# A graph network on one core: keys for the on-chip row picks kept in DRAM, blocks chosen by predicated copies

## The chip, the cores and the metric

The kernel runs on one core of a Trainium2 chip. The core has five engines, each with an instruction queue of its own: PE (matrix products into PSUM), DVE (vector operations), ACT (scalar operations, and it starts DMAs), POOL (it starts the indirect gathers) and SP (it starts most DMAs). The metric is the device time of one execution in microseconds. The time before is the median of three runs.

## The reference, cut to what matters

Three layers of a transformer convolution on a graph of N = 6250 nodes, with 206250 edges sorted by target node, D = 64 columns everywhere:

```python
q = x @ Wq + bq; k = x @ Wk + bk; v = x @ Wv + bv; e = edge_attr @ We
kj = k[src] + e
alpha = jnp.sum(q[dst] * kj, axis=-1) / jnp.sqrt(jnp.float32(D))
amax = jax.ops.segment_max(alpha, dst, num_segments=N)
p = jnp.exp(alpha - amax[dst])
w = p / jax.ops.segment_sum(p, dst, num_segments=N)[dst]
agg = jax.ops.segment_sum((v[src] + e) * w[:, None], dst, num_segments=N)
x = relu(agg + x @ Ws + bs)            # then a layer norm, but for the last layer
```

The last layer ends in a log-softmax, the input is added, and the sum is normalised.

## The kernel before, in words

The edges are cut into 403 chunks of 512 (T = 4 tiles of 128 edges), and four chunks are a batch, also called a unit: 100 full batches and a rest. A layer runs over its batches once. For one batch the work is:

- **fetch** (L556): SP loads the edges' attributes, 512 KB, into one of five `feat` buffers.
- **gather** (L578): for every tile of 128 edges POOL starts one indirect DMA that brings the 128 source rows of x (256 bytes each) into `feat`. A chunk's gathers are held by a small `gate` copy of its indices (L609, on ACT), made eight chunks ahead of the chunk that is being turned.
- **pick**: some tiles of a batch get their rows from the chip instead. In layer 0 an earlier sorting step has put the edges of each chunk in an order in which tile 0 holds only sources from the first RB = 18 blocks of 128 nodes, and tile 3 only from the last 18. Those blocks lie in SBUF as `parts`, split into two terms. A pick of one tile makes a one-hot and multiplies it with `parts`.
- **turn** (L1473, L1476): PE transposes a chunk's rows, and ACT copies them into `featT`.
- **scores** (L1484, L1488): PE adds a mask from the edges' position codes and the product of q and `featT` in the PSUM tile `ps_s`; DVE takes the maximum (L1498) and its negative (L1500), ACT the exponential `prob` (L1502).
- **weights** (L1510, L1512) transposes `prob` through the PSUM tile `ps_p`; **sums** (L1522, L1530) multiplies it with the rows; **store** (L1536) writes the partial result to DRAM.

A group of four node blocks is ended (`finish`: both partial results combined, output product, norm, next layer's projections) in about eight steps, one step in a batch, on DVE, PE and ACT between the other work. Layer 0 also sorts: products that permute the edge attributes (L983 makes the one-hot `hit` on DVE, L993 and L1002 multiply), `drain` (L1013, L1016, then the DMAs `toS` L1017 and `eaS` L1020 from ACT's queue), `index` (L1038: PE finds indices and block numbers of the sorted edges; DVE puts them into `src_b` and `kbs`) and the attributes transposed to `eaP`.

A pick runs so. `toS` holds for a batch 128 rows with the sorted edges' codes: position bits, and the source's node number split into h (its group of four blocks), its block within the group, and p (its row in the block). `decode` (L1608, on SP) loads this tile, 128 KB, three batches ahead. `Picker.aim` multiplies it with `coef` (L1182, one 128-column product for each pick): the product holds in every partition the key 128 h + p of each edge. One DVE operation (L1196) compares two picks' keys with `rank` in all NH = 5 groups h and gives `hot`, 128 x 5 x 256. `Picker.batch` multiplies (L1218: five groups by two terms, ten products a pick, 256 columns each but 128 for the last group) and so has for every edge the four candidate rows of its group. L1229 multiplies these with `which` (L1188, which of the four blocks it is), and two adds (L1232, L1233) put the row into `feat`. The products for keys go to PSUM tile `ps_m` in layers 1 and 2, to `ps_p` in layer 0; the candidates to one of two `ps_x` in layers 1 and 2, to the single `ps_s` in layer 0. Picks are taken two at a time, and `aim` for the next two is issued ahead of the products for the present two. `PICKS` sets how many tiles are picked: three a batch in layer 0 (one in the first ones), six in layers 1 and 2, so 13 and 10 gathers are left.

The order on each engine is the order in which the code is written: the main loop spreads picks, sorting and endings over the four turns of a batch.

Of the kernel before, what the change touches and what calls it, by code (L numbers as in the profile page):

```python
# [41 lines left out]
PICKS = ((3,), (6,), (6,))  # L42
LEAD = (4, 1, 1)


def slot(j):

    return j % 2 * (LB // 2) + j // 2
# [378 lines left out]
def main_path(  # L427
# [82 lines left out]
    tos = ctx.enter_context(tc.tile_pool(name="tos", bufs=4))  # L510
# [5 lines left out]
    gates = ctx.enter_context(tc.tile_pool(name="gates", bufs=6 * LB))  # L516
# [24 lines left out]
    toS = dram.tile([NT, P, CH], BF16, name="toS")  # L541
# [129 lines left out]
    def locate(k, m):  # L671

        half = CH // 2
        for i in range(2):
            at = slice(k * CH + i * half, k * CH + (i + 1) * half)
            room = picks.tile([P, NH, 2 * P], F32R, name="hot").rearrange("p h e -> p (h e)").bitcast(F32)
# [49 lines left out]
    fours = picks.tile([P, 2, KB, D], F32, name="rows_of_b", bufs=1).rearrange("p s b d -> p (s b d)")  # L726
# [20 lines left out]
    def widen(i):  # L747
# [3 lines left out]
        room = picks.tile([P, 2, KB, D], F32, name="rows_of_b", bufs=1).rearrange("p s b d -> p (s b d)")  # L751
# [70 lines left out]
    codeS = const.tile([P, P], BF16, name="codeS")  # L822
    coef = const.tile([P, LB, P], BF16, name="coef")
    pickc = const.tile([P, 2, LB], BF16, name="pickc")
    kbs = const.tile([P, NT, 2, LB], BF16, name="kbs")
# [3 lines left out]
    def tools():  # L829
# [4 lines left out]
        room = picks.tile([P, 2, KB, D], F32, name="rows_of_b", bufs=1).rearrange("p s b d -> p (s b d)")  # L834
        two, wide = room[:, :LB], room[:, P : 2 * P]
        at = [ident[:, i::W] for i in range(ROW_K + 1)]
        nc.vector.scalar_tensor_tensor(two, at[ROW_H], float(P), at[ROW_P], ALU.mult, ALU.add)
        nc.vector.tensor_copy(coef, two.unsqueeze(2).to_broadcast([P, LB, P]))
        nc.vector.scalar_tensor_tensor(pickc[:, 0], at[ROW_B], float(P), at[ROW_P], ALU.mult, ALU.add)
        nc.vector.tensor_copy(pickc[:, 1], at[ROW_K])  # L840
        nc.vector.memset(wide, 0.0)
        for j in range(LB):
            rows = slice(slot(j) * W, (slot(j) + 1) * W)
            nc.vector.tensor_copy(wide[rows, j * W : j * W + BITS + 1], bit[rows, :])
        pc = ps("a")
        nc.tensor.transpose(pc[:, :P], wide, ident)
        nc.vector.tensor_scalar(codeS, pc[:, :P], FAR, None, ALU.mult)
# [93 lines left out]
    class Move:  # L941
# [68 lines left out]
        def drain(self):  # L1010
# [6 lines left out]
            nc.scalar.dma_start(toS[self.k], self.to)  # L1017
# [15 lines left out]
        def index(self):  # L1033

            k = self.k
            pi = ps("a")[:, : T * 2 * LB].rearrange("p (t v c) -> p t v c", t=T, v=2)
# [15 lines left out]
            nc.vector.tensor_copy(kbs[:, k], pi[:, 0 :: T - 1, 1])  # L1052

# [99 lines left out]
    class Picker:  # L1153


        def __init__(self, layer):
            self.layer = layer
            self.todo = []
            for k in range(len(batches)):
                those = spots(picked(layer, k))  # L1160
                for t in (0, T - 1):
                    cs = [c for c, i in those if i == t]
                    self.todo += [(k, t, cs[i : i + 2]) for i in range(0, len(cs), 2)]
            self.aimed = []
            self.which = {}
            self.side = 0
            self.keys = ps("m") if layer else None

        def aim(self):

            if not self.todo or (self.layer, self.todo[0][0]) not in codes:
                return
            k, t, cs = self.todo.pop(0)
            n = len(cs)
            to = codes[self.layer, k]
            if self.layer:
                self.side = 1 - self.side
                pk = self.keys[:, self.side * 2 * P :][:, : n * P]
            else:
                pk = ps("p")[:, : n * P]  # L1180
            for s, c in enumerate(cs):
                nc.tensor.matmul(  # L1182
                    pk[:, s * P : (s + 1) * P], coef[:, c, :], to[:, t * P : (t + 1) * P], start=True, stop=True
                )
            if (self.layer, k) not in self.which:
# [9 lines left out]
            hot = picks.tile([P, NH, 2 * P], F32R, name="hot")[:, :, : n * P]  # L1195
            nc.vector.tensor_tensor(  # L1196
                hot,
                pk.unsqueeze(1).to_broadcast([P, NH, n * P]),
                rank.unsqueeze(2).to_broadcast([P, NH, n * P]),
                ALU.is_equal,  # L1200
            )
            self.aimed.append((k, t, cs, hot, self.which[self.layer, k]))

        def batch(self, k):
# [3 lines left out]
            while self.aimed and self.aimed[0][0] == k:  # L1208
                _, t, cs, hot, which = self.aimed.pop(0)
                self.aim()  # L1210
                n = len(cs)
                px = ps("x" if self.layer else "s").rearrange("p (s b d) -> p s b d", s=2, b=KB)
                b0 = RB if t else 0
                for s in range(n):
                    for m, h in enumerate((0, *reversed(range(1, NH)))):
                        w = min(KB, RB - h * KB)
                        for i in range(2):
                            nc.tensor.matmul(  # L1218
                                px[:, s, :w].rearrange("p b d -> p (b d)"),
# [5 lines left out]
                    if s + 1 < n:  # L1225
                        yield
                at = (LB if t else 0) + cs[0]
                rows = picks.tile([P, 2, KB, D], F32, name="rows_of_b", bufs=1)[:, :n]
                nc.vector.tensor_tensor(  # L1229
                    rows, px[:, :n], which[:, at : at + n, :].unsqueeze(3).to_broadcast([P, n, KB, D]), ALU.mult  # L1230
                )
                nc.vector.tensor_tensor(rows[:, :, : KB // 2], rows[:, :, : KB // 2], rows[:, :, KB // 2 :], ALU.add)  # L1232
                nc.vector.tensor_tensor(  # L1233
                    loaded[self.layer, k][:, cs[0] : cs[0] + n, t, 0], rows[:, :, 0], rows[:, :, 1], ALU.add
                )
                yield
# [176 lines left out]
    class Unit:  # L1413


        def __init__(self, layer, c, m):
# [6 lines left out]
            if self.placed:  # L1423
                self.to = codes[layer, self.k]
                return
# [406 lines left out]
```

## Time and profile before

| | |
|---|---|
| three runs | 4648.56 us median, 4645.43 to 4657.05 |
| the profiled execution | 4656.6 us; span 4654.9 us |
| granted TensorE clock | 0.966 on average |
| busy share of the span | PE 91%, DVE 82%, POOL 72%, ACT 43% |
| gathers | 3380 indirect DMAs, 0.96 us each in layers 1 and 2, 1.03 in layer 0 |
| layers 0, 1, 2 | their first gathers start at 5, 1982 and 3324 us |

A line of groups reads: source line, engine, operation, output tile <- input tiles, shapes, count | busy us in total, mean ns of one | idle time of the engine just before them, and what ended it. A timeline line reads: start us, length us, engine, line, operation, tiles, and in brackets the idle time before it with its releaser. Matmuls overlap, so their busy time is the time in which at least one is under way.

### The profile page before, as it was taken

To read this page: it belongs to the slowest core of one execution; us is meant where nothing else is said; L and a number is where in the kernel's file an instruction comes from. 1 tells how busy PE (TensorE), PEld (TensorE's weight loads), DVE (VectorE), ACT (ScalarE), POOL (GpSimd) and SP (SyncE) were. 2 spreads that over 40 slices of the span, in tenths; PEclk is the share of its full clock that TensorE was granted. 3 is DMA by queue.
4 is the path that set the end of the run, shared out by engine and by line. 5 is a ranking of instruction groups with operands and counts; after the bars stand their busy time and mean duration, and the time that the engine had idled before them with its cause. 6 is when DMAs were issued, how large, how long until landed. Compare 5 with 4: busy or idle time off the path is not lost.

```text
span 4654.9 us, 117245 instructions
## 1 busy us (share of the span) xinstructions
PE 4216.7 (91%) x41145; PEld 3111.6 (67%) x41145; DVE 3829.2 (82%) x9064; ACT 1995.7 (43%) x5733; POOL 3337.9 (72%) x3390
## 2 busy tenths in 40 slices
PE   6889999999999999689999999999699999999996
PEld 3445555555555555367888888887478778878874
DVE  6778888898888888478888888888478888888885
ACT  2455555555555555333333333333234333334443
POOL 6777777777777766277777777777477777777774
PEclk9999999999999999799999999999799999999997
DMA  8787777777777777445555565555356655656553
GB/s 188 192 210 184 188 204 188 189 195 200 199 198 193 192 197 189 125 102 132 137 139 137 138 144 138 140 138 129 86 128 143 141 135 135 138 130 143 136 135 81
DMA packets 769749, 725.47 MB, mean 156 GB/s; under 512 B 403478, under 2 KB 544880, under 8 KB 769156
## 3 DMA queue, kind: packets, MB, share of 16 engines
q1 hardware_dynamic: 572564, 480.73, 43.5%
q0 software_dynamic: 108160, 110.97, 12.7%
q10 hardware_dynamic: 88432, 126.17, 7.7%
q8 instruction: 334, 5.47, 0.5%
q14 instruction: 259, 2.12, 0.2%
HBM read 557.62 MB, written 159.87 MB: 154 GB/s over the span
## 4 chain that ended last, share of the span: by engine, by line


## 5 line engine op out<-in xcount | busy, mean ns | idle before, releaser
L578 POOL DMA_INDIRECT feat<-x,gate x2004 | 1924.4, 960 | 613.9 <-issue 471.5
L578 POOL DMA_INDIRECT feat<-in_x,gate x1328 | 1365.8, 1028 | 526.2 <-issue 317.1
L1218 PE MATMUL ps_x<-parts,hot 128*128 128x256 f32 (+1 forms) x11880 | 1567.1, 288 | 0.0
L1218 PEld LDWEIGHTS ps_x<-parts,hot 128*128 128x128 f32 x11880 | 1457.1, 193 | 0.0
L1476 ACT COPY featT<-ps_a 64x256 f32<-64x256 f32 x2380 | 872.4, 367 | 1305.8 <-PE ps_a L1473 1265.2
L1196 DVE TENSOR_TENSOR hot<-ps_m,rank 128x1280 fp32r<-128x1280 f32 x594 | 879.9, 1481 | 33.1 <-PE ps_m L1182 32.9
L993 PE MATMUL ps_x<-hit,thirds 128*64 128x512 bf16 x4800 | 637.7, 393 | 5.5 <-DVE hit L983 5.1
L1473 PE MATMUL ps_a<-ident,feat 128*128 128x128 f32 x2380 | 488.0, 283 | 64.0 <-DMA feat<-x,gate 40.4
L983 DVE TENSOR_SCALAR hit<-ruler,pos 128x512 bf16<-128x512 f16 x1600 | 504.6, 363 | 1.7 <-PE ps_m L1002 1.5
L1473 PEld LDWEIGHTS ps_a<-ident,feat 128*128 128x128 f32 x2380 | 281.9, 140 | 333.4 <-issue 287.5
L1229 DVE TENSOR_TENSOR rows_of_b<-ps_x,which 128x512 f32<-128x512 f32 x594 | 406.4, 684 | 88.1 <-PE ps_x L1218 87.1
L1502 ACT ACTIVATE prob<-ps_s,part 128x512 f32<-128x512 f32 (+1 forms) x306 | 210.6, 688 | 625.6 <-DVE part L1500 500.0
L1218 PE MATMUL ps_s<-parts,hot 128*128 128x256 f32 (+1 forms) x2680 | 392.3, 294 | 30.9 <-ACT prob L1502 30.9
L993 PEld LDWEIGHTS <-thirds 128*64 128x64 bf16 x4800 | 233.2, 111 | 230.5 <-issue 83.6
L1218 PEld LDWEIGHTS ps_s<-parts,hot 128*128 128x128 f32 x2680 | 340.8, 195 | 60.7 <-ACT prob L1502 40.7
L1498 DVE TENSOR_REDUCE most<-ps_s 128x1 f32<-128x512 f32 (+1 forms) x306 | 211.2, 690 | 189.4 <-PE ps_s L1488 181.4
L1232 DVE TENSOR_TENSOR rows_of_b<-rows_of_b 128x256 f32<-128x256 f32 (+1 forms) x776 | 321.0, 414 | 26.6
L1522 PE MATMUL ps_g<-feat,probT 128*32 128x128 f32 x9672 | 338.2, 279 | 4.1 <-DVE y L1366 2.3
L1488 PE MATMUL ps_s<-featT,q 128*32 128x512 f32 x2418 | 336.3, 611 | 5.9 <-ACT featT L1469 5.2
L1522 PEld LDWEIGHTS ps_g<-feat,probT 128*32 128x32 f32 x9672 | 263.5, 111 | 52.6 <-issue 34.0
L1512 DVE COPY probT<-ps_p 128x512 f32<-128x512 f32 (+1 forms) x306 | 209.2, 684 | 99.0 <-PE ps_p L1510 97.3
L1182 PEld LDWEIGHTS <-coef 128*128 128x128 bf16 x1456 | 134.7, 99 | 190.5 <-issue 175.1
(226 smaller groups left out, 4392.6 us busy)
## 6 DMA issues: line engine op xcount, KB each, us to landing
feat<-eaP SPq DMA_DIRECT2D x296, 512.0 KB
featT<-eaS SPq DMA_DIRECT2D x296, 512.0 KB
raw<-in_ea SPq DMA_DIRECT2D x200, 256.0 KB
eaS<-eT ACTq DMA_DIRECT2D x200, 256.0 KB
eaP<-eN ACTq DMA_DIRECT2D x200, 256.0 KB
to<-toS SPq DMA_DIRECT2D x296, 128.0 KB
feat<-x,gate POOLq DMA_INDIRECT x2004
feat<-in_x,gate POOLq DMA_INDIRECT x1328
```

Source lines behind the costliest of these rows:

```text
L578: nc.gpsimd.indirect_dma_start(out=feat[:, c, t, 0], out_offset=None, in_=xts[layer][:, :], in_offset=bass.IndirectOffsetOnAxis(ap=index[: ...
L983: nc.vector.tensor_scalar(hit, ruler, self.pos[:, at : at + 1], None, ALU.is_equal)
L993: nc.tensor.matmul(self.px[i][j * D : (j + 1) * D, :], self.thirds[i][:, part, (j * T + t) * D : (j * T + t + 1) * D], self.hits[t, 2 * i ...
L1196: nc.vector.tensor_tensor(hot, pk.unsqueeze(1).to_broadcast([P, NH, n * P]), rank.unsqueeze(2).to_broadcast([P, NH, n * P]), ALU.is_equal,)
L1218: nc.tensor.matmul(px[:, s, :w].rearrange("p b d -> p (b d)"), hot[:, h, s * P : (s + 1) * P], parts[:, i, b0 + h * KB : b0 + h * KB + w, ...
L1229: nc.vector.tensor_tensor(rows, px[:, :n], which[:, at : at + n, :].unsqueeze(3).to_broadcast([P, n, KB, D]), ALU.mult)
L1232: nc.vector.tensor_tensor(rows[:, :, : KB // 2], rows[:, :, : KB // 2], rows[:, :, KB // 2 :], ALU.add)
L1473: nc.tensor.transpose(pt[:, t // 2 * P : (t // 2 + 1) * P], rows[:, t * D : (t + 2) * D], ident)
L1476: nc.scalar.copy(featT[:, :, h, :], pt[h * D : (h + 1) * D, : T // 2 * P].rearrange("d (i e) -> d i e", e=P))
L1488: nc.tensor.matmul(self.p_s[slot(j) * W : (slot(j) + 1) * W, :], self.q[:, j * STRIDE : j * STRIDE + W], self.featT[:, j, :], start=False, ...
L1498: nc.vector.tensor_reduce(top[:n], self.p_s[:n], AX.X, ALU.max)
L1522: nc.tensor.matmul(p_g[rows, :].rearrange("n (h d) -> n h d", h=2), self.probT[:, t, rows], batch[:, c + j, t], start=(t == 0), stop=(t == ...
```

## The change

- `index` gets one more product: `keyc` (four columns) with the sorted codes gives the keys of tiles 0 and 3 of four chunks, 4 x 256. ACT copies them as fp16 and stores them in `keyS` in DRAM, 2 KB a batch.
- `decode` loads those keys of a batch, broadcast to 128 partitions (256 bytes for each pick in each partition), two or three batches ahead, behind the fourth turn. The `coef` products are gone.
- `aim` makes the one-hots of all picks of one tile kind of a batch (up to four) by five comparisons from SBUF, into two alternating buffers.
- The choice among four candidate rows is a copy of the first (on ACT in layers 1 and 2, on DVE in layer 0) and three predicated copies over it on DVE.
- `toS` keeps only the 24 rows of position codes that the scores need, written by four DMAs; each unit loads them itself, and `codeS` gives way to `codeT`.
- Picks in layers 1 and 2: 7, 6, 7 in turn. `tos` has two buffers, not four; `gates` 16, not 24.

The diff, without the three places where a scratch tile gets another name:

```diff
@@ -39,8 +39,9 @@
-PICKS = ((3,), (6,), (6,))
+PICKS = ((3,), (7, 6, 7), (7, 6, 7))
...
+MOST = max(n for p in PICKS for n in p)
@@ -507,13 +508,13 @@
-    tos = ctx.enter_context(tc.tile_pool(name="tos", bufs=4))
+    tos = ctx.enter_context(tc.tile_pool(name="tos", bufs=2))
...
-    gates = ctx.enter_context(tc.tile_pool(name="gates", bufs=6 * LB))
+    gates = ctx.enter_context(tc.tile_pool(name="gates", bufs=4 * LB))
@@ -538,7 +539,8 @@
-    toS = dram.tile([NT, P, CH], BF16, name="toS")
+    toS = dram.tile([NT, LB, BITS + 1, CH], BF16, name="toS")
+    keyS = dram.tile([NT, 2, LB, P], FP16, name="keyS")
@@ -819,10 +821,9 @@
     ones = const.tile([P, P], BF16, name="ones")
-    codeS = const.tile([P, P], BF16, name="codeS")
-    coef = const.tile([P, LB, P], BF16, name="coef")
+    keyc = const.tile([P, LB], BF16, name="keyc")
     pickc = const.tile([P, 2, LB], BF16, name="pickc")
-    kbs = const.tile([P, NT, 2, LB], BF16, name="kbs")
+    kbs = const.tile([P, NT, 2, LB], mybir.dt.uint8, name="kbs")
     four = const.tile([P, KB], F32, name="four")
@@ -831,20 +832,10 @@
         nc.vector.tensor_copy(four, ruler[:, :KB])
-        room = picks.tile([P, 2, KB, D], F32, name="rows_of_b", bufs=1).rearrange("p s b d -> p (s b d)")
-        two, wide = room[:, :LB], room[:, P : 2 * P]
         at = [ident[:, i::W] for i in range(ROW_K + 1)]
-        nc.vector.scalar_tensor_tensor(two, at[ROW_H], float(P), at[ROW_P], ALU.mult, ALU.add)
-        nc.vector.tensor_copy(coef, two.unsqueeze(2).to_broadcast([P, LB, P]))
+        nc.vector.scalar_tensor_tensor(keyc, at[ROW_H], float(P), at[ROW_P], ALU.mult, ALU.add)
         nc.vector.scalar_tensor_tensor(pickc[:, 0], at[ROW_B], float(P), at[ROW_P], ALU.mult, ALU.add)
         nc.vector.tensor_copy(pickc[:, 1], at[ROW_K])
-        nc.vector.memset(wide, 0.0)
-        for j in range(LB):
-            rows = slice(slot(j) * W, (slot(j) + 1) * W)
-            nc.vector.tensor_copy(wide[rows, j * W : j * W + BITS + 1], bit[rows, :])
-        pc = ps("a")
-        nc.tensor.transpose(pc[:, :P], wide, ident)
-        nc.vector.tensor_scalar(codeS, pc[:, :P], FAR, None, ALU.mult)
         for stamp in stamps:
@@ -1014,7 +1005,8 @@
                 nc.scalar.copy(self.eT[i], self.px[i])
-            nc.scalar.dma_start(toS[self.k], self.to)
+            for c in range(LB):
+                nc.scalar.dma_start(toS[self.k, c], self.to[c * W : c * W + BITS + 1])
             for i in range(2):
@@ -1033,7 +1025,12 @@
             k = self.k
-            pi = ps("a")[:, : T * 2 * LB].rearrange("p (t v c) -> p t v c", t=T, v=2)
+            pa = ps("a")
+            pi = pa[:, : T * 2 * LB].rearrange("p (t v c) -> p t v c", t=T, v=2)
+            pk = pa[:LB, 2 * P :].rearrange("c (t e) -> c t e", t=2)
+            nc.tensor.matmul(
+                pk, keyc, self.to.rearrange("r (t e) -> r t e", t=T)[:, :: T - 1], start=True, stop=True
+            )
             for t in range(T):
@@ -1050,6 +1047,9 @@
             nc.vector.tensor_copy(kbs[:, k], pi[:, 0 :: T - 1, 1])
+            key = small.tile([LB, 2, P], FP16, name="key", bufs=1)
+            nc.scalar.copy(key, pk)
+            nc.scalar.dma_start(keyS[k].rearrange("t c e -> c t e"), key)
@@ -1160,28 +1160,18 @@
                     cs = [c for c, i in those if i == t]
-                    self.todo += [(k, t, cs[i : i + 2]) for i in range(0, len(cs), 2)]
+                    self.todo += [(k, t, cs)] if cs else []
             self.aimed = []
             self.which = {}
-            self.side = 0
-            self.keys = ps("m") if layer else None
+            self.turn = 0
...
-            if not self.todo or (self.layer, self.todo[0][0]) not in codes:
+            if not self.todo or (self.layer, self.todo[0][0]) not in keys:
                 return
...
             n = len(cs)
-            to = codes[self.layer, k]
-            if self.layer:
-                self.side = 1 - self.side
-                pk = self.keys[:, self.side * 2 * P :][:, : n * P]
-            else:
-                pk = ps("p")[:, : n * P]
-            for s, c in enumerate(cs):
-                nc.tensor.matmul(
-                    pk[:, s * P : (s + 1) * P], coef[:, c, :], to[:, t * P : (t + 1) * P], start=True, stop=True
-                )
+            first = LB * P if t else 0
             if (self.layer, k) not in self.which:
@@ -1192,13 +1182,13 @@
                 self.which[self.layer, k] = which
-            hot = picks.tile([P, NH, 2 * P], F32R, name="hot")[:, :, : n * P]
-            nc.vector.tensor_tensor(
-                hot,
-                pk.unsqueeze(1).to_broadcast([P, NH, n * P]),
-                rank.unsqueeze(2).to_broadcast([P, NH, n * P]),
-                ALU.is_equal,
-            )
+            room = (LB, MOST - LB)[self.turn]
+            hot = picks.tile([P, NH, room * P], F32R, name=f"hot{self.turn}", bufs=1)[:, :, : n * P]
+            self.turn = 1 - self.turn
+            for h in range(NH):
+                nc.vector.tensor_scalar(
+                    hot[:, h], keys[self.layer, k][:, first : first + n * P], rank[:, h : h + 1], None, ALU.is_equal
+                )
             self.aimed.append((k, t, cs, hot, self.which[self.layer, k]))
@@ -1208,32 +1198,33 @@
                 self.aim()
-                n = len(cs)
-                px = ps("x" if self.layer else "s").rearrange("p (s b d) -> p s b d", s=2, b=KB)
                 b0 = RB if t else 0
-                for s in range(n):
+                for s, c in enumerate(cs):
+                    if s % 2 == 0:
+                        n = min(2, len(cs) - s)
+                        px = ps("x" if self.layer else "s").rearrange("p (s b d) -> p s b d", s=2, b=KB)
                     for m, h in enumerate((0, *reversed(range(1, NH)))):
...
                             nc.tensor.matmul(
-                                px[:, s, :w].rearrange("p b d -> p (b d)"),
+                                px[:, s % 2, :w].rearrange("p b d -> p (b d)"),
                                 hot[:, h, s * P : (s + 1) * P],
...
                             )
-                    if s + 1 < n:
-                        yield
-                at = (LB if t else 0) + cs[0]
-                rows = picks.tile([P, 2, KB, D], F32, name="rows_of_b", bufs=1)[:, :n]
-                nc.vector.tensor_tensor(
-                    rows, px[:, :n], which[:, at : at + n, :].unsqueeze(3).to_broadcast([P, n, KB, D]), ALU.mult
-                )
-                nc.vector.tensor_tensor(rows[:, :, : KB // 2], rows[:, :, : KB // 2], rows[:, :, KB // 2 :], ALU.add)
-                nc.vector.tensor_tensor(
-                    loaded[self.layer, k][:, cs[0] : cs[0] + n, t, 0], rows[:, :, 0], rows[:, :, 1], ALU.add
-                )
-                yield
+                    if s % 2 == n - 1:
+                        at = (LB if t else 0) + c - n + 1
+                        found = loaded[self.layer, k][:, c - n + 1 : c + 1, t, 0]
+                        copy = nc.scalar.copy if self.layer else nc.vector.tensor_copy
+                        copy(found, px[:, :n, 0])
+                        for b in range(1, KB):
+                            nc.vector.copy_predicated(
+                                found,
+                                which[:, at : at + n, b].bitcast(I32).unsqueeze(2).to_broadcast([P, n, D]),
+                                px[:, :n, b],
+                            )
+                    yield
@@ -1420,13 +1411,9 @@
             self.plain = not layer and not self.placed
-            if self.placed:
-                self.to = codes[layer, self.k]
-                return
             self.to = tos.tile([P, CH], BF16, name="to")
-            nc.sync.dma_start(
-                self.to[: m * (BITS + 1), :], places[c : c + m].rearrange("c b e -> (c b) e")
-            )
+            here = toS[self.k] if self.placed else places[c : c + m]
+            nc.sync.dma_start(self.to[: m * (BITS + 1), :], here.rearrange("c b e -> (c b) e"))
@@ -1480,10 +1467,7 @@
             self.p_s = ps("s")
-            if self.placed:
-                nc.tensor.matmul(self.p_s, codeS, self.to, start=True, stop=False)
-            else:
-                nc.tensor.matmul(self.p_s[:n], codeT[:k, :n], self.to[:k, :], start=True, stop=False)
+            nc.tensor.matmul(self.p_s[:n], codeT[:k, :n], self.to[:k, :], start=True, stop=False)
             for j in range(self.m):
@@ -1599,13 +1583,17 @@
-    codes = {}
+    keys = {}
...
-        if k < NT and placed(layer, k) and (layer, k) not in codes and (layer or k in moved):
-            codes[layer, k] = tos.tile([P, CH], BF16, name="to")
-            nc.sync.dma_start(codes[layer, k], toS[k])
+        n = picked(layer, k) if k < NT else 0
+        if n and (layer, k) not in keys and (layer or k in moved):
+            keys[layer, k] = picks.tile([P, MOST * P], FP16, name="keys", bufs=2)
+            nc.sync.dma_start(
+                keys[layer, k][:, : n * P],
+                keyS[k].rearrange("t c e -> (t c e)")[: n * P].partition_broadcast(P),
+            )
@@ -1684,8 +1672,6 @@
             chunks[layer, u + 1].across()
-            for k in range(u + 1, u + 4):
-                decode(layer, k)
             if layer:
@@ -1722,6 +1708,8 @@
             move(pace)
+            for k in range(u + 2, u + 4):
+                decode(layer, k)
```

## The prediction

> **What bounds the kernel now.** I first cut the span by stage with the table of stretches (PE, PEld, DVE, ACT, POOL busy us with instructions, then granted clock, DMA share, GB/s): a steady piece of layer 0, of layer 1 and of layer 2.
>
> ```profile
> 600.00:1800.00 1200.00, 1124.85 (x11138) 686.44 (x11134) 1046.39 (x3148) 641.71 (x1639) 864.86 (x852) 0.99 0.77 195
> 2300.00:3200.00 900.00, 858.36 (x8683) 723.58 (x8675) 783.25 (x1437) 340.50 (x1118) 683.11 (x712) 1.00 0.59 138
> 3400.00:4500.00 1100.00, 1031.94 (x10420) 877.39 (x10412) 949.99 (x1748) 430.93 (x1384) 835.02 (x869) 0.99 0.60 137
> ```
>
> PE is busy 94 to 95% in all three, DVE 86 to 87%. The groups of the layer 1 stretch (count, busy, mean ns, idle before and its releaser), POOL's and PE's:
>
> ```profile
> L578 POOL DMA_INDIRECT feat<-x,gate x712 | 683.7, 960 | 217.1 <-issue 163.8 <-DMA feat<-x,gate 28.7 <-ACT gate L609 10.4
> L1182 PE MATMUL ps_m<-to,coef 128*128 128x128 bf16 x426 | 58.4, 218 | 40.4 <-DVE hot L1196 40.0
> ```
>
> 426 coefficient products are 71 batches of six picks, so a batch takes 900/71 = 12.68 us. A gather comes every 900/712 = 1.264 us, and ten to a batch are 12.64: POOL has no free time. PE works 858.36/71 = 12.09 of the 12.68, and nearly all its idle time (40.0 of 41.6 us, 0.56 a batch) is one wait. The timeline of PE and DVE shows it:
>
> ```profile
> 2603.60 2.61 PE L1218 MATMUL ps_x<-parts,hot 128*128 128x256 f32 x20
> 2606.04 0.38 PE L1473 MATMUL ps_a<-ident,feat 128*128 128x128 f32 x2
> 2607.68 0.27 PE L1182 MATMUL ps_m<-to,coef 128*128 128x128 bf16 x2 [1.25 <-DVE hot L1196]
> ```
> ```profile
> 2603.43 0.69 DVE L1498 TENSOR_REDUCE most<-ps_s 128x1 f32<-128x512 f32 x1 [0.60 <-PE ps_s L1488]
> 2604.21 0.15 DVE L1500 TENSOR_SCALAR part<-most 128x1 f32<-128x1 f32 x1
> 2604.28 1.22 DVE L1334 TENSOR_TENSOR w<-both,mm 128x1024 f32<-128x1024 f32 x1
> 2605.53 0.69 DVE L1337 TENSOR_TENSOR w<-w 128x512 f32<-128x512 f32 x1
> 2606.14 1.48 DVE L1196 TENSOR_TENSOR hot<-ps_m,rank 128x1280 fp32r<-128x1280 f32 x1
> 2607.54 0.68 DVE L1229 TENSOR_TENSOR rows_of_b<-ps_x,which 128x512 f32<-128x512 f32 x1
> ```
>
> DVE comes to the one-hot late, because 1.86 us of a node group's ending stand ahead of it, and PE waits. So in layers 1 and 2 three things lie within 5% of each other: POOL's pace, PE's work, and this DVE lump. Fewer gathers alone cannot bring the 10 to 9.33 that the counts suggest (0.84 us a batch): PE takes the saved gathers over.
>
> Layer 0: three picks a batch, so 196 coefficient products are 65.3 batches of 18.4 us. POOL needs 13 gathers of 1.264, 16.4. From its groups and ACT's timeline:
>
> ```profile
> L1510 PE MATMUL ps_p<-ident,prob 128*128 128x128 f32 x264 | 43.3, 286 | 17.1 <-DVE hot L1196 17.1
> L1182 PE MATMUL ps_p<-to,coef 128*128 128x128 bf16 x196 | 33.7, 226 | 3.3 <-DVE probT L1512 3.1
> ```
> ```profile
> 1205.53 0.33 ACTq L1017 DMA_DIRECT2D toS<-to  x1
> 1206.02 0.84 ACTq L1020 DMA_DIRECT2D eaS<-eT  x2
> 1206.90 0.27 ACT L1530 COPY part<-ps_g 128x128 f32<-128x128 f32 x1 [0.42 <-ACT eT L1016]
> 1208.59 0.69 ACT L1502 ACTIVATE prob<-ps_s,part 128x512 f32<-128x512 f32 x1 [1.42 <-DVE part L1500]
> ```
>
> PE waits there because keys and probabilities share one PSUM buffer (ps_p). ACT has 1.84 us idle between its drain and the exponential.
>
> **Layers 1 and 2, per batch.** PE loses six coefficient products. A pair starts 0.09 us ahead of the first pick product (2603.51 to 2603.60) and lasts 0.22; I take 0.16, three pairs 0.48. PE gains two thirds of a pick: 20 products take 2.44 us (2603.60 to 2606.04), so a pick is 1.22 and the gain 0.81. PE's work becomes 12.09 - 0.48 + 0.81 = 12.42 in layer 1. In layer 2 it was 1031.94/86.9 = 11.87 (869 gathers, ten a batch) of 12.66, and becomes 12.20.
>
> The stall: today PE reaches its second group 0.25 (turn) + 2.44 + 0.25 = 2.9 us after the scores, DVE has the next one-hot at 0.85 (maximum and its negative) + F + 1.40, F being the ending's work. F over 0.65 stalls; F = 1.86 gives 1.2, the 1.25 seen. Afterwards the one-hots are made from SBUF, a half batch ahead, and what is late next is the product buffer: the third group needs the first one's selection, at 0.85 + F + 1.8 (five compares) + 1.0 (three predicated copies) = 3.65 + F, and PE comes to it at about 5.3. So F may reach 1.65. I leave 0.15 of the 0.59 in layer 1, and 0.35 of the 0.79 in layer 2, whose endings are longer. 12.57 and 12.55: -0.11 each, on 99 batches of two layers -22 us. With no stall left it is -(0.26 + 0.46) x 99 = -71; with all of it, +65.
>
> The prices in that chain. Compare (tensor_scalar with a pointer, fp16 in, four-byte out, SBUF), by duration min/median/max of two rows:
>
> ```profile
> L983 DVE TENSOR_SCALAR hit<-ruler,pos x1600: 218/345/578, 58.8 to 1910.0; 128x512 bf16<-128x512 f16 x178
> L1369 DVE TENSOR_SCALAR y<-y x39: 226/321/495, 380.1 to 4643.2; 128x256 f32<-128x256 f32 x33, 128x192 f32<-128x192 f32 x3, 128x128 f32<-128x128 f32 x3
> ```
>
> For 512 columns it lies between 0.345 (two-byte result) and 0.69 (copy of 512 f32, L1512). Where columns go one by one, one costs 1.045 ns (1481 less 812 ns, for 640 columns of L1196). The f32 row's fastest are 0.226 for its 128 columns, 0.259 for 192 and 0.293 for 256: 0.52 ns a column on 0.16; a pointer operand adds 0.055 (L1395, 64 columns, 0.247). So I take 0.48 for four picks, 0.41 for three, 0.34 for two, each about 0.05 less from start to start, since they overlap (four of 0.345 take 1.28 us at 1205.23 in layer 0). A batch: 3.6 to 4.0 against 3 x 1.48 = 4.44. The Trainium skill (VectorE: DVE Perf Modes, The perf-mode tier table) lets an fp32 tensor_scalar of SBUF run at twice the rate of an fp32 tensor_tensor or of a PSUM operand; 0.52 against 1.045 ns agrees. At the slower rate, by this page what the old form pays, the sum would be that of rival (2). Predicated copy, 128 columns: no row has one; between a 128 x 128 copy (ACT's 0.27) and twice the tensor_tensor of that size (L1233, 298 ns). I take 0.30 and the 0.03 gap of dependent instructions, eleven a batch: 3.6 against 3 x 1.41 = 4.22. The first copy goes to ACT: 3.7 x 0.27 = 1.0 us on an engine 38% busy. DVE falls from 11.03 to about 9.8.
>
> POOL: 9.33 x 1.264 = 11.80, under PE. Keys: a load of up to 0.23 MB a batch for 0.13, and one small load more, at a DMA share of 0.6: nothing. They stand on SP at a batch's end and wait for the compares of two batches earlier, done by mid-batch; behind them stands the next feat load, which waits for PE anyway. Gates 24 to 16: at most eight ahead and four in work, nothing.
>
> **Layer 0, per batch.** PE loses two coefficient groups, 0.32, their wait 0.05, and ps_p's wait 17.1/65.3 = 0.26. It gains the key product, between a pickc product (16.5/264 = 0.06) and a 512-column one (0.38): 0.15. ACT gains a copy (0.37) and four DMA issues of 0.33 to 0.42; in the built order the last of six issues in a row uses the semaphore of the first again, and so waits for its landing. Most fits into the 1.84 idle; I let 0.1 through (none, to 2). DVE drops 0.5, hidden. Net -0.38, 96 batches: -36.
>
> Sum -58 on the profiled execution's 4656.6: 4598.6. The median shown is 8.0 lower, so 4590.
>
> **Rivals.** (1) POOL stays the pace. In layer 0, where 16 fast compares a batch run beside the gathers, these average 1016 ns, not 960; 0.09 more each gives 9.33 x 1.354 = 12.64, and layers 1 and 2 gain nothing: -36, 4612. And L1369 at 256 columns takes 0.293 in layer 0, mostly 0.43 to 0.495 in layers 1 and 2, so fast compares and gathers do hold each other up. Against it: the median gather is 947 ns in both stages, and the layer 0 mean gives only 9.33 x 1.32 = 12.3, under PE's 12.4. The Trainium skill (SBUF — State Buffer, Who interferes with whom) says that such a compare locks GpSimd out of a shared port for its whole length, and the other way round; this speaks against the change, and both rows agree. (2) DVE becomes the bound. Besides one-hot and selection it has 11.03 - 8.66 = 2.4, and 0.88 of waits at scores and transposes (62.5/71) that it can't fill; the point is 9.4 us for both. Compares at one column per cycle are 6.0, with copies at 0.38 from start to start 4.2: 13.5 a batch, +155 in layers 1 and 2, less 36: 4768. With 9.7 us for both it is 4668. Copies of 0.6 alone do the same. (3) All stalls go, layer 0 keeps 0.48: -71 - 46, 4532. (4) ACT's queue eats layer 0's gain (0.6 a batch gets through instead of 0.1): -22 + 12, 4639, no change.
>
> **Numbers.** Forecast 0.38, (1) 0.20, (2) 0.20, (3) 0.12, (4) 0.10. About 0.3% (14 us) can be told from no change. Faster: forecast, (1) and (3), less 0.03 that fall short, 0.67; same 0.11; slower 0.22. The range reaches from under (3) to the lower prices of (2): 4510 to 4700.
>
> **What would show it.** Right: no PE wait for a one-hot, compares near 0.4, predicated copies near 0.3, POOL with gaps, batches of about 12.55 in layers 1 and 2 and 18.0 in layer 0. Wrong: gathers back to back with a mean over 1.0 (1); DVE over 93% busy (2); PE idle behind ACT's exponential or ps_a in layer 0 (4).

## The result, and the profile after

The changed kernel takes 4709.86 us (median of 6 runs, 4701.55 to 4722.78), the kernel before 4651.97 (6 runs): ratio 1.0126, 95% interval 1.0108 to 1.0144. So it is slower by 1.3%, where 4590 was forecast. The profiled execution took 4702.4 us, with a span of 4700.6 (before: 4654.9) and a granted clock of 0.961 (0.966). Four of the kernels below were first run in a session in which every kernel took 38% longer, the kernel before too (6420.1 us), and there one store came to 0.9952 of it, two buffers to 0.9951, four stores in the old kernel to 1.0215 and the key path to 1.0025; only the later runs of these four, labelled _2, are used.

DVE takes one maximum a batch (L1498 before, L1482 after), 306 in all, so the two traces can be laid side by side, maximum by maximum. The changed kernel is 7.0 us late at the 8th, 83.7 at the 92nd, 95.9 at the 106th, early in layer 1, 70.0 at the 204th, its end, and 45.9 at the last. Over 84 batches of each layer, in us a batch:

| | before | forecast | after |
|---|---|---|---|
| layer 0 | 18.36 | 17.98 | 19.28 |
| layer 1 | 12.68 | 12.57 | 12.42 |
| layer 2 | 12.65 | 12.55 | 12.37 |

Layers 1 and 2 gained 50 us, over twice the 22 that were forecast. Layer 0 lost 95 where it should have gained 36. The table of stretches of the kernel after (PE, PEld, DVE, ACT, POOL busy us with instructions, granted clock, DMA share, GB/s):

```profile
600.00:1800.00 1200.00, 1114.71 (x10518) 667.62 (x10518) 955.84 (x3295) 632.53 (x1626) 866.63 (x817) 0.97 0.69 180
2300.00:3200.00 900.00, 893.84 (x8877) 765.22 (x8876) 675.08 (x2094) 407.04 (x1405) 685.24 (x687) 1.00 0.61 149
3400.00:4500.00 1100.00, 1067.41 (x10599) 917.63 (x10600) 812.51 (x2545) 511.65 (x1731) 837.11 (x843) 0.99 0.60 145
```

In layer 1 PE is busy 99.3% (95.4% before) and DVE has fallen from 87 to 75%: the stall is gone. In layer 0 PE is no busier than before, gets less done (10518 products for 11138), and its clock is lower, 0.97 for 0.99. The groups of the layer 1 stretch, POOL's and DVE's:

```profile
L580 POOL DMA_INDIRECT feat<-x,gate x687 | 686.1, 999 | 215.0 <-issue 151.5 <-ACT gate L611 13.8 <-DMA feat<-x,gate 12.8
...
L1222 DVE COPY_PREDICATED feat<-which,ps_x 128x128 f32<-128x128 int32 x652 | 195.5, 301 | 119.0 <-ACT feat L1220 99.2 <-issue 3.7
L1189 DVE TENSOR_SCALAR hot<-keys,rank 128x512 fp32r<-128x512 f16 x360 | 151.6, 487 | 0.0
L1189 DVE TENSOR_SCALAR hot<-keys,rank 128x384 fp32r<-128x384 f16 x245 | 87.8, 422 | 0.0
L1189 DVE TENSOR_SCALAR hot<-keys,rank 128x256 fp32r<-128x256 f16 x120 | 37.3, 375 | 0.0
```

Compares of 0.487, 0.422 and 0.375 us and predicated copies of 0.301: the prices taken were 0.48, 0.41, 0.34 and 0.30. A gather has gone from 0.960 to 0.999. What PE waits for in that stretch (us in total, times, longest), where 40.0 us stood for the one-hot:

```profile
PE ps_x L1209 <- DVE feat L1222: 5.8, 11, 0.8
```

An ending's lump now stands ahead of compares that PE needs half a batch later, as PE's and DVE's timelines show:

```profile
2610.95 2.61 PE L1209 MATMUL ps_x<-parts,hot 128*128 128x256 f32 x20
2613.39 0.38 PE L1460 MATMUL ps_a<-ident,feat 128*128 128x128 f32 x2
2613.53 2.60 PE L1209 MATMUL ps_x<-parts,hot 128*128 128x256 f32 x20
```
```profile
2611.95 1.24 DVE L1293 TENSOR_SCALAR y<-y,mv,dev 128x64 f32<-128x64 f32 x4
2613.22 0.89 DVE L1298 TENSOR_TENSOR y<-y,gb 128x256 f32<-128x256 f32 x2
2614.03 1.81 DVE L1189 TENSOR_SCALAR hot<-keys,rank 128x256 fp32r<-128x256 f16 x5
2615.75 1.83 DVE L1222 COPY_PREDICATED feat<-which,ps_x 128x128 f32<-128x128 int32 x6
```

Layer 0 (600 to 1800 us), PE's groups for the shared buffers: the wait at L1494 (17.1 us before, L1510) is gone, but L1209 waits for the selection, and the endings' products wait for L1514, the drain of ps_g on ACT:

```profile
L1209 PE MATMUL ps_s<-parts,hot 128*128 128x256 f32 x1880 | 280.4, 298 | 35.8 <-DVE feat L1222 18.3 <-ACT prob L1486 17.5
...
L1494 PE MATMUL ps_p<-ident,prob 128*128 128x128 f32 x252 | 41.3, 286 | 0.0
...
L1268 PE MATMUL ps_g<-ws,xT 64*128 64x65 f32 x64 | 11.7, 337 | 17.3 <-ACT part L1514 17.3
...
L1354 PE MATMUL ps_g<-ve,wT 128*128 128x64 f32 x56 | 8.6, 302 | 8.6 <-ACT part L1514 8.6
```

ACT's timeline after its drain, and PE's beside it:

```profile
1202.84 0.63 ACTq L1009 DMA_DIRECT2D toS<-to  x2
...
1203.50 0.66 ACTq L1009 DMA_DIRECT2D toS<-to  x2
1204.95 1.97 ACTq L1012 DMA_DIRECT2D eaS<-eT  x2
1206.96 0.27 ACT L1514 COPY part<-ps_g 128x128 f32<-128x128 f32 x1 [3.17 <-DMA toS<-to]
1208.87 0.69 ACT L1486 ACTIVATE prob<-ps_s,part 128x512 f32<-128x512 f32 x1 [1.64 <-DVE part L1484]
```
```profile
1204.91 0.44 PE L1460 MATMUL ps_a<-ident,feat 128*128 128x128 f32 x2
1207.28 1.10 PE L1354 MATMUL ps_g<-ve,wT 128*128 128x64 f32 x8 [1.94 <-ACT part L1514]
...
1211.45 2.50 PE L1209 MATMUL ps_s<-parts,hot 128*128 128x256 f32 x10
```

The four `toS` issues take 1.3 us, then the two of `eaS` hold ACT's queue for 1.97 us (0.84 before): in this batch the second waits until the first `toS` store, whose semaphore it is to use, has landed. The drain that stands behind it starts 3.17 us after ACT's last work, and PE stands idle for 1.94 us. Then ten pick products take 2.50 us, which take 1.22 elsewhere: the clock records put TensorE at half rate from 1209.3 to 1216.1.

### The profile page after: what moved, and what is told of

The parts are those of the page before. It is cut to its first block, busy times and chain, and to the rows that moved or that the text cites. A ratio compares the mean times of both kernels' runs of the same rounds, so it can differ in the third digit from the quotient of the medians.

```text
span 4700.6 us, 121008 instructions
## 1 busy us (share of the span) xinstructions
PE 4320.8 (92%) x41108; PEld 3192.2 (68%) x41108; DVE 3447.4 (73%) x11319; ACT 2197.6 (47%) x6559; POOL 3325.4 (71%) x3258
## 4 chain that ended last, share of the span: by engine, by line
## 5 line engine op out<-in xcount | busy, mean ns | idle before, releaser
L580 POOL DMA_INDIRECT feat<-x,gate x1872 | 1862.3, 995 | 614.3 <-issue 403.1
L580 POOL DMA_INDIRECT feat<-in_x,gate x1328 | 1414.1, 1065 | 572.3 <-issue 311.8
L1209 PE MATMUL ps_x<-parts,hot 128*128 128x256 f32 (+1 forms) x13200 | 1712.9, 286 | 32.5 <-ACT feat L1220 16.6
L1209 PEld LDWEIGHTS ps_x<-parts,hot 128*128 128x128 f32 x13200 | 1604.8, 191 | 53.8 <-ACT feat L1220 32.5
L1189 DVE TENSOR_SCALAR hot<-keys,rank 128x384 fp32r<-128x384 f16 (+3 forms) x2460 | 916.4, 437 | 0.0
L1222 DVE COPY_PREDICATED feat<-which,ps_x 128x128 f32<-128x128 int32 (+1 forms) x2178 | 617.1, 288 | 377.9 <-ACT feat L1220 314.5
L984 PE MATMUL ps_x<-hit,thirds 128*64 128x512 bf16 x4800 | 650.7, 398 | 6.1 <-DVE hit L974 6.1
L1460 PE MATMUL ps_a<-ident,feat 128*128 128x128 f32 x2380 | 483.2, 284 | 31.4 <-DMA feat<-x,src_b 21.4
L1460 PEld LDWEIGHTS ps_a<-ident,feat 128*128 128x128 f32 x2380 | 280.5, 141 | 297.2 <-issue 270.9
L1220 ACT COPY feat<-ps_x 128x128 f32<-128x128 f32 (+1 forms) x726 | 186.4, 257 | 629.2 <-PE ps_x L1209 619.8
L1209 PE MATMUL ps_s<-parts,hot 128*128 128x256 f32 (+1 forms) x2680 | 404.6, 300 | 57.8 <-ACT prob L1486 33.9
L1209 PEld LDWEIGHTS ps_s<-parts,hot 128*128 128x128 f32 x2680 | 348.3, 199 | 119.9 <-issue 71.5
L984 PEld LDWEIGHTS <-thirds 128*64 128x64 bf16 x4800 | 237.1, 112 | 236.4 <-issue 89.7
L1482 DVE TENSOR_REDUCE most<-ps_s 128x1 f32<-128x512 f32 (+1 forms) x306 | 211.2, 690 | 227.7 <-PE ps_s L1472 221.1
L611 ACT COPY gate<-src_b 128x4 int32<-128x4 int32 x1185 | 227.1, 192 | 0.0
```

Source lines behind the costliest of these rows:

```text
L580: nc.gpsimd.indirect_dma_start(out=feat[:, c, t, 0], out_offset=None, in_=xts[layer][:, :], in_offset=bass.IndirectOffsetOnAxis(ap=index[: ...
L611: copy(gate, index[:, i : i + T])
L984: nc.tensor.matmul(self.px[i][j * D : (j + 1) * D, :], self.thirds[i][:, part, (j * T + t) * D : (j * T + t + 1) * D], self.hits[t, 2 * i ...
L1189: nc.vector.tensor_scalar(hot[:, h], keys[self.layer, k][:, first : first + n * P], rank[:, h : h + 1], None, ALU.is_equal)
L1209: nc.tensor.matmul(px[:, s % 2, :w].rearrange("p b d -> p (b d)"), hot[:, h, s * P : (s + 1) * P], parts[:, i, b0 + h * KB : b0 + h * KB + ...
L1222: nc.vector.copy_predicated(found, which[:, at : at + n, b].bitcast(I32).unsqueeze(2).to_broadcast([P, n, D]), px[:, :n, b],)
```

## The experiments

Theory A was that this queue makes layer 0 late. Rival B was the selection: the one ps_s is held for about 1.2 us (a copy and three predicated copies) where it was free after the multiply of 0.69. Rival C was the key product with its copy and store.

In the listings below the line numbers of the edited kernels differ by a few.

**One store of `to`** (after):

```diff
-    toS = dram.tile([NT, LB, BITS + 1, CH], BF16, name="toS")
+    toS = dram.tile([NT, P, CH], BF16, name="toS")
-            for c in range(LB):
-                nc.scalar.dma_start(toS[self.k, c], self.to[c * W : c * W + BITS + 1])
+            nc.scalar.dma_start(toS[self.k], self.to)
-            here = toS[self.k] if self.placed else places[c : c + m]
+            here = toS[self.k].rearrange("(c w) e -> c w e", w=W)[:, : BITS + 1] if self.placed else places[c : c + m]
```

> The changed kernel with the rows of `to` stored whole, in one DMA of 128 rows instead of four of six; the load picks the 24 rows out of it. Theory A (ScalarE's queue: the last of six issues in a row waits until the first has landed, the drain of ps_g behind it is late, PE stalls and its clock is halved for 3.4 us or more after it): the 143 us that L1514 waits for toS and eaS in layer 0 go, half-clock time in layer 0 falls from 177 us towards 102, and layer 0 gives back 60 to 95 of the 94 us it lost: 4615 to 4650 us. Theory B (the selection holds ps_s for 1.2 us instead of 0.69, so PE's next pick products are late): no change, 4700 to 4715. Theory C (key product, its copy and its store): 4700 to 4715.

Measured: 4648.62 us (ratio to before 0.9985, 0.9976 to 0.9995), 61 us less than the change; layer 0 18.66 us a batch. No wait of the drain for `toS` or `eaS` is left, and PE's wait for the drain falls from 30.5 to 1.3 us in layer 0. Half-clock time, counted from the third to the 98th maximum, falls from 150 to 106 us (before: 75). Theory A holds for two thirds of the loss.

**Two product buffers in layer 0** (after):

```diff
-                        px = ps("x" if self.layer else "s").rearrange("p (s b d) -> p s b d", s=2, b=KB)
+                        px = ps("x" if self.layer else "sp"[s // 2]).rearrange("p (s b d) -> p s b d", s=2, b=KB)
```

> The changed kernel with the third pick's products of layer 0 put into ps_p instead of ps_s, so that they need not wait for the selection of the first two. Theory A: at most the 24 us that PE waits there for L1222, and little of it in the end, since ACT is late anyway: 4685 to 4710. Theory B: the 24 us and the half-clock time behind them, 40 to 70 us: 4640 to 4670. Theory C: no change.

Measured: 4703.31 (1.0105, 1.0082 to 1.0128), 7 us less than the change, less than the two intervals tell apart. Half of the wait for the selection only changes its place, to L1494, and PE waits for DVE elsewhere, at L984, as well:

```profile
PE ps_x L984 <- DVE hit L974: 21.2, 29, 1.1
...
PE ps_p L1494 <- DVE feat L1222: 12.9, 21, 0.6
```

Rival B, as a matter of that buffer, falls: of its 24 us of waits little is got back. What the selection costs layer 0 as a whole, this run does not show.

**Four stores in the kernel before:**

```diff
-            nc.scalar.dma_start(toS[self.k], self.to)
+            for c in range(LB):
+                nc.scalar.dma_start(toS[self.k, c * W : (c + 1) * W], self.to[c * W : (c + 1) * W])
```

> The kernel before with its one store of `to` made four of 32 rows each (the same bytes). Theory A: the wait appears in the old kernel too, and layer 0 loses 50 to 95 us: 4700 to 4745, layers 1 and 2 as before (12.67 us a batch). Theories B and C: three issues of 0.33 us into 1.84 us of idle ACT, 4650 to 4660.

Measured: 4829.84 (1.0373, 1.0356 to 1.0390), 176 us more, all of it in layer 0 (20.20 us a batch; layers 1 and 2 12.65). ACT's waits in layer 0, of which the kernel before has none:

```profile
ACT part L1531 <- DMA toS<-to: 201.6, 50, 6.0
...
ACT part L1531 <- DMA eaS<-eT: 81.6, 19, 6.8
```

The hold on ACT's queue appears in a kernel without any other part of the change, and at about twice the upper end of the forecast; these stores are 32 KB each, those of the change 6 KB.

**Two stores** (after, with `toS` as in the first experiment):

```diff
-            nc.scalar.dma_start(toS[self.k], self.to)
+            for c in range(0, LB, 2):
+                nc.scalar.dma_start(toS[self.k, c * W : (c + 2) * W], self.to[c * W : (c + 2) * W])
```

> The changed kernel with the rows of `to` stored whole in two DMAs of 64 rows (one store gave 4648.6 us, four of six rows 4709.9). If the loss comes from the last of six issues waiting for the landing of the first (eight transfers may be in flight), four issues in a row do not reach it: 4645 to 4660 us, no wait of L1514 for toS. If every further issue on ScalarE costs its share (61 us over three), 4665 to 4675.

Measured: 4656.88 (1.0012, 1.0001 to 1.0023). Going from one store to two costs 0.27% by the ratios, 13 us, and from two to four 1.14%, 53 us. So the number of issues alone does not explain it; what the first 13 us are was not looked into. The drain waits 2.8 us for `toS` in the whole layer, once.

The semaphore numbers in the traces tell what ACT's issues wait for. The DMAs that ACT and SP start take eight semaphores (counters that tell that a transfer has landed) in turn, 433 or 434 issues on each in the changed kernel, and an issue is held until the transfer that had its semaphore eight issues before has landed. The holds of over 0.2 us ahead of these stores add up to 4 us in the kernel before, 15 with one store, 3 with two, 100 in the changed kernel and 162 in the old kernel with four stores. Theory A named the batch's own first store. That is only a third of it: its semaphore comes up again within the six issues in 62 of 100 batches, and 31 of the 100 us are spent on it. Of the rest 34 are spent on SP's load of `feat` (14 batches, 2.5 us each) and 29 on SP's load of `raw`, the attributes to be sorted. In the old kernel with four stores 154 of the 162 us are spent on the load of `feat`, in 73 batches, and under 1 us on `toS`. The names in the wait lists above are inferred and do not show this.

**Key path alone** (before, with the product, the copy and the store of `index` added as in the change, and `kbs` in one byte; nothing reads the keys):

```diff
+            nc.tensor.matmul(
+                pk, keyc, self.to.rearrange("r (t e) -> r t e", t=T)[:, :: T - 1], start=True, stop=True
+            )
...
+            key = small.tile([LB, 2, P], mybir.dt.float16, name="key", bufs=1)
+            nc.scalar.copy(key, pk)
+            nc.scalar.dma_start(keyS[k].rearrange("t c e -> c t e"), key)
```

> The kernel before with the key product, its copy on ScalarE and its store added in layer 0 (stored and never read), and kbs in one byte. If these are the rest of what layer 0 lost (the changed kernel with one store is still 0.30 us a batch behind), 25 to 40 us: 4680 to 4695. If they are hidden, as ACT's copy and the store were priced, only the product shows, 0.15 to 0.22 us a batch: 4668 to 4675. If nothing of it shows, 4650 to 4660 and the rest lies in the selection and the products.

Measured: 4684.14 (1.0063, 1.0043 to 1.0084), 33 us more; layer 0 18.77 us a batch, 0.41 more. That is what the change with one store still lacks in layer 0 (0.30), and a little over (the change also gains something there, as the next section works out). PE waits 8.4 us for the copy, and each product adds about 0.23 us to PE's work, some 21 us in all. Rival C holds for the last third.

**Six picks** (after: `PICKS = ((3,), (6,), (6,))`):

> The changed kernel with six picks a batch in layers 1 and 2 again (ten gathers, as in the kernel before); layer 0 is as in the changed kernel. If the gathers stay as slow beside the fast compares as they are in the changed kernel (0.999 us and a gap of 0.305), ten of them are 13.0 us and POOL sets the pace: 0.6 us a batch more on 198 batches, 4830 us. If a gather goes back to 0.96 (12.64 a batch): 4755. If PE is all that counts (12.33 less 0.81 of work): 11.6 us a batch and 4550.

Measured: 4822.75 (1.0350, 1.0320 to 1.0381); layers 1 and 2 12.96 and 12.99 us a batch. POOL's group and PE's wait, 2400 to 3300 us:

```profile
L580 POOL DMA_INDIRECT feat<-x,gate x695 | 689.0, 991 | 211.9 <-issue 153.4 <-DMA feat<-x,gate 20.1 <-ACT feat L1220 10.7
```
```profile
PE ps_a L1460 <- DMA feat<-x,gate: 67.5, 57, 3.0
```

900/695 = 1.295 us a gather, ten to a batch: POOL sets the pace and PE waits for its gathers.

**More picks in the kernel before** (`PICKS = ((3,), (7, 6, 7), (7, 6, 7))`):

> The kernel before with 6.67 picks a batch in layers 1 and 2, all else as it was (keys by products on PE, selection by multiply and add). PE's work rises from 12.09 to 12.95 us a batch in layer 1: with no stall left 13.0 and with all of the old 0.56 left 13.5, so 4715 to 4820 us. If instead the fewer gathers are what brought the 0.25 us a batch in layers 1 and 2: 4600. Layer 0 as before (18.36 us a batch) in either case.

Measured: 4809.92 (1.0331, 1.0306 to 1.0356); 13.63 and 13.34 us a batch, PE still waiting 45 us for the one-hot in 900. So in layers 1 and 2 neither half of the change gains alone: the faster selection without the picks costs 0.3 us a batch, the picks without the faster selection 0.7 to 0.95, and both together save 0.25 to 0.28.

**Slow compares, six picks** (the kernel of six picks with each one-hot made by one operation from the same keys):

```diff
-            for h in range(NH):
-                nc.vector.tensor_scalar(
-                    hot[:, h], keys[self.layer, k][:, first : first + n * P], rank[:, h : h + 1], None, ALU.is_equal
-                )
+            nc.vector.tensor_tensor(
+                hot,
+                keys[self.layer, k][:, first : first + n * P].unsqueeze(1).to_broadcast([P, NH, n * P]),
+                rank.unsqueeze(2).to_broadcast([P, NH, n * P]),
+                ALU.is_equal,
+            )
```

> The changed kernel with six picks in layers 1 and 2 (4822.8 us, POOL's pace 1.295 us a gather) and the five compares of a one-hot made one tensor_tensor of the same keys from SBUF, which is slower on VectorE. If the fast compares and gathers hold each other up, gathers go back to 1.26 from start to start and a batch to 12.65 us: about 4755, unless VectorE (9.4 us busy and some 1.7 more) becomes late. If they do not, the gathers stay at 1.295 and the time at 4820 or above.

Measured: 5267.04 (1.1325, 1.1287 to 1.1363), a miss both ways: the gathers did not recover, they went to 1.230 us, and DVE is busy only 62% of the layer 1 stretch. POOL's timeline and DVE's:

```profile
2708.21 0.94 POOL L580 DMA_INDIRECT feat<-x,gate  x1 [0.30 <-issue]
2709.45 3.51 POOL L580 DMA_INDIRECT feat<-x,gate  x1 [0.30 <-ACT gate L611]
2713.26 0.94 POOL L580 DMA_INDIRECT feat<-x,gate  x1 [0.30 <-issue]
```
```profile
2709.32 2.82 DVE L1188 TENSOR_TENSOR hot<-keys,rank 128x2560 fp32r<-128x2560 f16 x1
```

A gather that starts within such a compare ends about 0.8 us after it (384 of 397). Taking the DVE operation that runs 0.15 us into each gather of layers 1 and 2, and what the gather takes beyond 0.944 us: beside the old compare (keys in PSUM) 0.003 us more on average, beside the five compares of the change 0.15, beside this one 1.15. The Trainium skill (SBUF — State Buffer, Who interferes with whom) says that a VectorE operation contends with GpSimd when it runs in a two-port mode or, where GpSimd reads SBUF, when two of its inputs lie there, and not otherwise; the three numbers agree. The same section infers that a two-input operation would not hold up the making of DMA descriptors; if that is what a gather does on POOL, the gather of 3.51 us speaks against it.

**A better version: one store of eT** (one store of `to`, two product buffers, and eT as one tile with one DMA):

```diff
+            eT = sorts.tile([P, 2, CH], F32, name="eT", bufs=1)
...
+            nc.scalar.dma_start(
+                eaS[self.c0 : self.c0 + LB].rearrange("(i c) d e -> (c d) i e", i=2), eT
+            )
```

> One store of `to`, the second product buffer (4644.0 us), and the two stores of eT made one DMA: two issues in a row on ScalarE instead of six. If issues and transfers in flight still hold ScalarE's copies up in layer 0, 10 to 25 us less: 4620 to 4634. If what is left there is PE's own work, 4640 to 4648.

Measured: 4643.31 (0.9985, 0.9975 to 0.9995). The same two edits without the merged store:

> One store and the second product buffer together, the version that should beat both kernels. Theory A: little more than the one store alone, 4600 to 4640. Theory B: little more than the second buffer alone, 4640 to 4670. If each stands for its own part of the loss: 4580 to 4615.

4643.98 (0.9977, 0.9963 to 0.9991). The two are alike: with the holds gone, fewer issues bring nothing that can be told apart. Half-clock time in layer 0 is back at 75 and 79 us. Two variants of the merged one:

> The version with one store of `to`, one of eT and two product buffers (4643.3 us), with seven and six picks in turn, 6.5 a batch, in layers 1 and 2 instead of 6.67. PE's work there falls by 0.2 us to 12.2 and 12.0 a batch, but POOL's gathers rise from 9.33 to 9.5, at 1.30 to 1.31 us from start to start 12.35 to 12.45. If POOL's pace counts as well as PE's: a batch of 12.4 to 12.5, 4640 to 4660. If PE alone counts: 12.25, 4610.

4637.55 (0.9947, 0.9926 to 0.9967): 12.34 and 12.33 us a batch, and a gather every 1.299 us, 9.5 of them 12.34. POOL's gathers now follow one another with no gap beyond their usual 0.30 us, and PE is still busy 98.9% of the layer 1 stretch, so the two are level; the forecast batch of 12.4 to 12.5 was at least 0.06 too slow. This is the best of all the kernels, 0.5% ahead of the kernel before.

> The same version (4643.3 us) with 6.67 picks and the copy of the keys in layer 0 made by VectorE instead of ScalarE. If the copy on ScalarE, which stands behind a VectorE operation and holds ps_a for the next transposes, is part of what the key path costs: the 10 us that PE waits for it, 4628 to 4638. If the product itself and what it displaces on PE are all of it: 4638 to 4648.

4666.61 (1.0009, 0.9999 to 1.0019), a miss: PE still waits 6.4 us for the key's copy (8.6 with the copy on ScalarE), and now also for gathers (32.0 us at L1460 in layer 0, which the version with the copy on ScalarE does not show). How DVE's copy makes them late was not looked into.

## Why the prediction was wrong, by its own steps

- **Layer 0, "I let 0.1 through (none, to 2)"**: the step that failed. The mechanism was named (the last of six issues waits for the landing of the first) and it came, as a third of a larger hold: SP's loads share the eight semaphores, and the issues wait for them too. And it was costed on ACT's idle time of 1.84 us, read as lying between the drain and the exponential; by the two rows shown there only 0.42 lies ahead of the drain, and 1.42 behind it. Four stores instead of one cost 0.62 us a batch (19.28 less 18.66). What was left out is who waits behind ACT: the drain of ps_g stands after the issues, PE's next ending products need ps_g, and a PE stall of 2 us costs again through the clock. From the third to the 98th maximum the 92 us lost are 35 of PE idle time, half of the 75 us more at half clock, and 20 of PE's work. Idle gaps over 1.5 us were 17 before, 44 after. The forecast missed layer 0 by 1.30 us a batch (0.92 lost for 0.38 gained): 0.52 by this step, 0.26 and 0.52 by the next two.
- **Layer 0, key product 0.15**: with its copy and store 0.41, by the key path alone. The product is about 0.23; the copy priced as hidden holds ps_a.
- **Layer 0, the gains of 0.32 + 0.05 + 0.26**: 19.28 - 18.36 - 0.62 - 0.41 leaves a gain of 0.11. The wait of ps_p did go; the selection's wait on ps_s took its place. Of the 0.32 of coefficient products PE got little back: in the version with one store and two buffers a pick product adds 0.141 us to PE's work instead of 0.133, and a position-code product 0.32 instead of 0.22. With 30 pick products a batch that is 0.24 and 0.10 more work, against three coefficient products of 0.13. A likely reason is that the coefficient products had been filling the start of the group behind them; it was not tested.
- **Rival (4)** was this mechanism, given 0.6 us a batch, just what was measured, and a chance of 0.10. No row stands behind the 0.6, so that it fits is luck, and its sign did not come: PE idled behind the drain of ps_g, not behind the exponential or ps_a. Its sum of 4639 and the forecast's both failed on the other two terms, which it left at 0.15 and -0.63.
- **Layers 1 and 2, -0.11 each**: right in kind, too small. The stall fell from 0.59 and 0.78 to 0.09 and 0.37 us a batch (forecast 0.15 and 0.35). PE's work rose by 0.25 and 0.14, not 0.33. The picks' part was right: alone in the kernel before they add 0.85 and 0.77 (forecast 0.81 and 0.05 for their key product). So by difference what left PE, the coefficient pairs above all, was worth 0.60 to 0.63, where 0.48 and that 0.05 were taken.
- **Compares and copies**: right, by the rows above, and DVE at 9.3 us busy a batch instead of 9.8. Rival (2) did not come in this kernel.
- **POOL and rival (1)**: POOL is the near second that was feared. Gathers of layer 1 start every 1.312 us on average, 14 longer gaps in 795 gathers included, and 9.33 make 12.25 of the 12.42. Rival (1) priced 1.354. The kernel with six picks shows what the longer gathers cost: 12.96 a batch where the same ten gathers made 12.68 before.

## What to carry to other kernels

Before a DMA is split, list what stands behind its issues on that engine, and count the transfers in flight, those of every engine that shares the semaphores: the issue that comes round to a semaphore whose transfer has not landed holds up everything behind it. A stall in the engine that sets the pace costs more than its length if its clock falls, so price both: here 35 us of idle time came with 37 of slower work. Where two engines run within a few per cent of each other, a change must relieve both: here the picks and the selection each made the kernel slower alone and faster together.

## What the runs showed of the hardware

TensorE's clock falls without a fully idle window. The records hold it at half rate for stretches of 3.41 us or multiples. In layer 0 of the kernel after, from the third to the 98th maximum, 21 of the 31 falls come at the end of a 3.41 us window in which PE was busy less than half of the time, and only 1 of 469 other full-clock windows was that idle. The other ten falls come after windows that were busy up to 67%, as 27 windows without a fall were too. The stall of 1.94 us above was enough: its window was 58% busy. The Trainium skill (TensorE: Matmul & The Clock Gate, What's actually happening) puts the fall after at least one idle window of about 3.4 us. The length of the window agrees; that it must be idle does not.

A compare reading its keys from SBUF as a two-input operation holds a gather up until it ends (3.51 us beside one of 2.82; 1.15 us more on average), far more than five short ones of the same work (0.15 us on average). Transfers of one engine can hold up another engine's queue: 154 us of ACT's time in the old kernel with four stores went to landings of SP's `feat` loads.
